# One row preparation at a time, v's sums ahead of q's turning, and PSUM tiles at fixed banks in the second input stage of a transformer block

## The chip, the cores and the metric

The kernel runs on one core of one Trainium2 chip. A core has a matrix engine (TensorE, PE in the profile, with its weight loads shown apart as PEld), a vector engine (VectorE, DVE), a scalar engine (ScalarE, ACT), a general engine (GpSimd, POOL) and a queue that here only issues DMAs (SyncE, SP). Each engine takes its own instructions in their order and waits on semaphores for the others. TensorE writes its results to PSUM, which holds eight banks of 128 x 512 float32 values; all else lies in SBUF or in DRAM.

The metric is the device time of one execution in microseconds (us); lower is better.

## The reference

The reference is one block of a conditioned transformer on x of shape 2 x 2048 x 576 in float32, with 16 heads of 36 values:

```python
mod = jax.nn.silu(c) @ w_ada + b_ada
sh_msa, sc_msa, g_msa, sh_mlp, sc_mlp, g_mlp = jnp.split(mod, 6, axis=1)
xn = _ln(x, 1e-06) * (1 + sc_msa[:, None, :]) + sh_msa[:, None, :]
qkv = (xn @ w_qkv + b_qkv).reshape(B, N, 3, H, hd)
q, k, v = (qkv[:, :, 0], qkv[:, :, 1], qkv[:, :, 2])
q = _ln(q, 1e-05, qn_g, qn_b)
k = _ln(k, 1e-05, kn_g, kn_b)
attn = jax.nn.softmax(jnp.einsum('bqhd,bkhd->bhqk', q, k) * scale, axis=-1)
o = jnp.einsum('bhqk,bkhd->bqhd', attn, v).reshape(B, N, C)
x = x + g_msa[:, None, :] * (o @ w_proj + b_proj)
xn2 = _ln(x, 1e-06) * (1 + sc_mlp[:, None, :]) + sh_mlp[:, None, :]
h = jax.nn.gelu(xn2 @ w1 + b1, approximate=False)
x = x + g_mlp[:, None, :] * (h @ w2 + b2)
```

## The kernel before

The two batch elements go one after the other through three stages: the inputs (normed x times w_qkv, then the norm of each head of q and k), the attention, and the output projection. The MLP follows for both at once. The change touches the input stage of the second element, its border to the attention, and the PSUM pool that this stage shares with the first element's output projection.

**The second input stage** is `in_pairs` (L1327). Tokens come in tiles of 128, sixteen of them. Tiles 0 and 1 are done singly; then seven pairs follow, t0 = 2, 4, ... 14, called pair 2 to pair 14 below. A pair makes three products in the order k, q, v, each of two token tiles by 576 columns. `seven_products` (L1195) computes each from seven smaller matrix products by a Strassen scheme, in four groups: (1,), (2, 6), (5, 7), (4, 3). The figures name the small products. Each group takes one PSUM tile from `s_tile()`, of two banks, so that the four groups of one product fill all eight banks, and group n of a product needs the tile that group n of the product before has left.

**What empties the tiles** is `combined` (L1233): an ACT copy of product 1, and five DVE sums `do[0]` to `do[4]` (L1248 to L1252). `do[0]` reads the group (2, 6). `do[1]` reads both banks of the group (5, 7). `do[2]` reads product 4, `do[3]` product 5 and `do[4]` product 3. So the tile of (5, 7) is free once `do[3]` is done, and that of (4, 3) after `do[4]`.

**What follows for k and q** is `finishing` (L1279): square (ACT, L1287), sum per head (DVE, L1291), root (ACT, L1294), reciprocal (DVE) and scaling (POOL, L1300), and `turned_out` (L1302). The last transposes in blocks of 32 on DVE (L1304) and writes the result to DRAM by eight DMAs (L1307): seven on SP and one on POOL. Then it reads rows back for the attention. For k that is `take_k_block` (L875), called with four tiles in pairs 2, 6 and 10 and with two tiles in pairs 12 and 14; it issues four DMAs on SP (L812 for `km`, L814 for `ke`). For q it is `take_q(0, 0)` in pair 2 alone, eight DMAs on SP. All of these wait until the writes have landed. The names `kt` and `qt` in the code stand for this last step of k and of q.

**A row preparation** is what is left to be done on DVE once the rows are back. For a block of k it is one function: `scaled` of `km` and `parted` of `ke`, four instructions (L847, L847, L856, L857). For q it is two functions: `scaled` of `qm` (one instruction), and `parted` of `qe` (three). The functions wait in the list `taken`.

**The order of the work** is written out by hand in this stage: DVE, SP, POOL and ACT, like PE, take their instructions in the order of the code. In a pair the order on DVE, seen from the lines in `in_pairs`, is this. First come what the pair before left (`rest`: v's `do[2]` to `do[4]` and q's `qt`), then k's five sums, and after q's products k's sum per head, q's `do[0]`, and `kd`. There q's `do[1]` and the call `rows_made()` (L1389) stand, which runs all that `taken` holds; then `kt`, q's `do[2]` to `do[4]`, and after v's products q's sum per head, v's `do[0]`, `qd` and v's `do[1]`. In the last pair `qt` stands ahead of v's `do[2]` to `do[4]` (L1404).

**The border.** The attention's PSUM pool has eight single banks in the place of the four tiles; its first four score matmuls (L1519) take banks 0 to 3. A bank can be written once the last reader of what lay there is done.

Of the kernel before, what the change touches and what calls it, by code (L numbers as in the profile page):

```python
# [8 lines left out]
F32 = mybir.dt.float32  # L9
# [7 lines left out]
P = 128  # L17
# [14 lines left out]
def dit_block(  # L32
# [26 lines left out]
    B, N, C = x.shape  # L59
# [16 lines left out]
    psum = {}  # L76

    @contextmanager
    def psum_pools():
        with (  # L80
# [2 lines left out]
        ):  # L83
            yield

    def s_tile():
        return psum["s"].tile([P, 2, 512], F32, tag="s", name="s")

    def bank():
# [6 lines left out]
    def opened(name, bufs=1, side="left"):  # L96

        stack = ExitStack()
        pool = stack.enter_context(tc.tile_pool(name=name, bufs=bufs, side=side, reuse_waits="tile"))
        return pool, stack.close  # L100

    def opened_psum(**bufs):

        stack = ExitStack()
        for n, count in bufs.items():
            psum[n] = stack.enter_context(
                tc.tile_pool(name=f"ps_{n}", bufs=count, space=PSUM, reuse_waits="tile")
            )

        def close():  # L110
            stack.close()
            for n in bufs:
                del psum[n]

        return close
# [636 lines left out]
    def block_of_small():  # L752
# [13 lines left out]
        def outs_opened():  # L766
            outs, close = opened("outs", side="right")
            held["qo"] = outs.tile([P, NKC, N], F32, name="qo")
            held["spare"] = outs.tile([P, 11, C], F32, name="spare")
            spare[:] = [held["spare"][:, i, :] for i in range(11)]  # L770
            nc.gpsimd.memset(held["spare"][0:1, :, 0:1], 0.0)
            return close
# [294 lines left out]
        def input_modulated(b, xnt):  # L1067
            turned_modulated(xnt, slice(0, P), 0, b)
            return xnt
# [12 lines left out]
        def inputs(b, weights, making, work, xnts, turned, loaded):  # L1082

            wq, wq4, bq = weights
            both, squares, taken = {}, {}, []
# [44 lines left out]
            def product(w, t, ps=None, steps=(0, 1)):  # L1130

                ps = ps or s_tile()
                full, parts, _ = xnts[t]
                for a in range(2):
                    f = slice(w * C + a * HALF, w * C + (a + 1) * HALF)
                    out_a = ps[:, a, :HALF]
                    for k in range(FULL) if 0 in steps else ():
                        nc.tensor.matmul(out_a, full[:, k, :], wq[:, k, f], start=k == 0, stop=False)  # L1138
                    for i in range(2) if 1 in steps else ():
                        nc.tensor.matmul(out_a, parts[:, i, :], wq4[:, f], start=False, stop=i == 1)  # L1140
                return ps
# [35 lines left out]
            def bias_rows():  # L1177

                spread = work.tile([P, 3, 2, HALF], F32R, name="bias_rows")
                ones = work.tile([P, P], F32R, name="ones")  # L1180
                nc.gpsimd.memset(spread.bitcast(F32), 0.0)
                nc.gpsimd.memset(ones.bitcast(F32), 0.0)
                nc.gpsimd.memset(ones[0:2, :].bitcast(F32), 1.0)
                value, up = ended[0:2, :HALF], high[0:2, :HALF]
                for w in range(3):
                    first, second = (bq[0:2, w * C + a * HALF : w * C + (a + 1) * HALF] for a in range(2))
                    nc.vector.tensor_tensor(value, second, first, ALU.subtract)
                    for a, part in enumerate((first, value)):
                        nc.vector.tensor_scalar(up, part, sign_q[0:2, :], None, ALU.mult)
                        nc.vector.scalar_tensor_tensor(  # L1190
                            spread[0:2, w, a, :], part, low_q[0:2, :], up.bitcast(F32), ALU.mult, ALU.add
                        )
                return spread, ones
# [74 lines left out]
            def features_begun(t):  # L1268
                if t < NT and t not in xnts:
                    xnts[t] = input_loaded(turned.pop(t), nc.gpsimd, work if t % 4 == 3 else None)  # L1270

            def pair_opened(w, t0):
                pairs[w] = work.tile([P, 2, C], F32, name="pair", bufs=4)
                both.update({(w, t0 + t): pairs[w][:, t, :] for t in range(2)})
# [46 lines left out]
                return squares_made, summed_up, rooted, divided, turned_out  # L1321

            def rows_made():
                while taken:
                    taken.pop(0)()

            def in_pairs():  # L1327

                sums = work.tile([P, 4, 2, 3, HALF], F32, name="weight_sums")
                less = work.tile([P, 3, HALF], F32R, name="wq4_less")  # L1330
                nc.sync.dma_start(out=less.bitcast(F32), in_=saved["less"])
                for w in (1, 0, 2):
                    nc.sync.dma_start(out=sums[:, :, :, w, :], in_=saved["sums"][:, :, :, w, :])
                spread, ones = bias_rows()

                for w in (1, 0):
                    pair_opened(w, 0)
                features_begun(3)
                k = product(1, 0)
                biased(1, k, 0)  # L1340
                q = product(0, 0)
                biased(0, q, 0)
                v = product(2, 0)
                biased(2, v, 0)
                k = product(1, 1)
                biased(1, k, 1)
                input_modulated(b, xnts[3])
                more = token_sums(2)
                ks, kr, kq, kd, kt = finishing(1, 0)
                ks(), kr(), kq(), kd()  # L1350
                q = product(0, 1)
                biased(0, q, 1)
                qs, qr, qq, qd, qt = finishing(0, 0)
                qs(), qr(), qq()
                kt()
                qd()
                v = product(2, 1)
                biased(2, v, 1)
                rest = [qt]

                for t0 in range(2, NT, 2):
                    last = t0 == NT - 2
                    operands = sums, less, spread, ones, more
                    for t in range(2):
                        features_begun(t0 + 2 + t)

                    pair_opened(1, t0)
                    do, copied = combined(1, t0, seven_products(1, t0, operands))
                    copied()
                    for step in rest:  # L1370
                        step()
                    do[0]()
                    do[1]()
                    do[2](), do[3](), do[4]()
                    ks, kr, kq, kd, kt = finishing(1, t0)
                    ks()

                    pair_opened(0, t0)
                    do, copied = combined(0, t0, seven_products(0, t0, operands))
                    copied()  # L1380
                    kr(), kq()
                    do[0]()
                    kd()
                    if not last:
                        for t in range(2):
                            input_modulated(b, xnts[t0 + 2 + t])
                        more = token_sums(t0 + 2)
                    do[1]()
                    rows_made()  # L1389
                    kt()  # L1390
                    do[2](), do[3](), do[4]()
                    qs, qr, qq, qd, qt = finishing(0, t0)
                    qs()

                    do, copied = combined(2, t0, seven_products(2, t0, operands))
                    copied()
                    qr(), qq()
                    do[0]()
                    qd()
                    do[1]()  # L1400
                    if not last:
                        rest = [*do[2:], qt]
                        continue
                    qt()  # L1404
                    do[2](), do[3](), do[4]()
                    return taken

            modulated = {0}
# [28 lines left out]
            if b > 0:  # L1437
                return in_pairs()
# [57 lines left out]
            taken = key_rows[-2:]  # L1496
# [220 lines left out]
        close_psum = opened_psum(s=4)  # L1717
# [7 lines left out]
        for b in range(B):  # L1725
# [5 lines left out]
                left = inputs(b, weights, making, work, xnts, turned, loaded)  # L1731
            close_weights()
            close_work()
            close_outs = outs_opened()
            att, close_att = opened("att")
            close_psum()
            close_psum = opened_psum(b=8)
# [63 lines left out]
                attend(b, att, hooks, left)  # L1801
            close_att()
            close_psum()
            close_psum = opened_psum(s=4)
            wp, close_wp = opening["wp"]
            if b + 1 < B:
                weights, close_weights, making = kept_weights()
# [85 lines left out]
        for j in range(TPB + 1):  # L1893
            n, i = divmod(j, TPB)
# [172 lines left out]
        close_psum = opened_psum(s=4)  # L2067
# [98 lines left out]
    with tc.If(is_small > 0) as branch:  # L2166
        with tc.manual_schedule(engines={mybir.EngineType.PE}):
            block_of_small()
# [34 lines left out]
```

## Time and profile before

| | us |
|---|---|
| median of three runs | 3138.34 (3137.75 to 3140.68) |
| the profiled execution's own time | 3137.95 |
| its span in the trace | 3136.0 |
| TensorE busy in it | 3103.5 |
| DVE busy | 1569.0 |
| first matmul of the second input stage | at 1085.4 |
| first score matmul of the second attention | at 1291.8 |

Times "at" are us from the start of the span. A row of the timeline gives the start, the duration, the engine, the line, the operation, the tile written and those read, and in brackets how long the engine sat idle before and who ended it; rows of one kind that follow each other are merged with a count (x4), and a matmul of float32 stands there twice. SPq is the queue that issues DMAs: its rows show the issue, not the transfer. A window's row gives the busy time and instructions of each engine, and the clock that TensorE was granted (1.00 is full speed).

### The profile page before, as it was taken

How to read it: one execution, taken by the hardware profiler on the slowest of the kernel's cores; microseconds unless marked ns; L12 is line 12 of the kernel's file. 1: busy time of each engine (PE TensorE's matmuls, PEld its weight loads, DVE VectorE, ACT ScalarE, POOL GpSimd, SP SyncE). 2: the span in 40 equal slices, each digit the busy share in tenths (PEclk: the TensorE clock that was granted, in tenths of full speed). 3: DMA queues.
4: the chain of work that ended last, by engine and by line, in shares of the span. 5: the costliest groups of instructions: out<-in, count | busy, mean ns of one | idle time of the engine just before them, and what ended most of it. 6: DMA issues, size and time to landing. Idle time of an engine off the chain costs nothing. (4 is left out here: it accounts for less than half of the span.)

```text
span 3136.0 us, 47001 instructions
## 1 busy us (share of the span) xinstructions
PE 3103.5 (99%) x17511; PEld 1853.4 (59%) x17511; DVE 1569.0 (50%) x2287; ACT 1477.0 (47%) x2853; POOL 718.7 (23%) x1005
## 2 busy tenths in 40 slices
PE   8999999999999999999999999999999999999999
PEld 6883333333333778533333333368888888777777
DVE  6773444444443556444434444355565553545454
ACT  2336666766667023466666666633565541000000
POOL 4650100132321355200011110013333320212111
PEclk9999999999999999999999999999999999999999
DMA  5773332233342644311122321146554434333331
GB/s 146 188 144 85 104 89 57 70 97 96 91 112 56 223 96 77 84 46 34 46 57 74 85 68 57 56 168 188 159 145 130 128 110 167 106 121 122 113 106 39
DMA packets 294838, 324.65 MB, mean 104 GB/s; under 512 B 168904, under 2 KB 225160, under 8 KB 292488
## 3 DMA queue, kind: packets, MB, share of 16 engines
q1 hardware_dynamic: 246464, 198.32, 22.0%
q0 software_dynamic: 46960, 117.92, 14.4%
q10 hardware_dynamic: 1176, 5.31, 0.5%
q8 instruction: 141, 2.31, 0.3%
q14 instruction: 97, 0.79, 0.1%
HBM read 200.50 MB, written 110.43 MB: 99 GB/s over the span
## 5 line engine op out<-in xcount | busy, mean ns | idle before, releaser
L1523 ACT ACTIVATE pt<-b 128x512 f32<-128x512 f32 x2048 | 1057.3, 610 | 483.8 <-PE b L1532 267.6
L1532 PE MATMUL b<-pt,vt 128*64 128x512 f32 x4096 | 935.0, 598 | 1.8 <-ACT pt L1523 1.8
L1532 PEld LDWEIGHTS b<-pt,vt 128*64 128x64 f32 x4096 | 271.8, 136 | 583.9 <-issue 437.7
L1519 PE MATMUL b<-qm,km 32*128 32x512 f32 x4096 | 564.0, 615 | 3.0 <-issue 3.0
L1584 DVE TENSOR_TENSOR ot<-b,ot 128x512 f32<-128x512 f32 x192 | 132.8, 692 | 587.8 <-PE b L1532 587.8
L1519 PE MATMUL b<-qe,ke 16*128 16x512 f32 x2048 | 421.7, 793 | 0.0
L1519 PEld LDWEIGHTS b<-qm,km 32*128 32x128 f32 x4096 | 192.4, 185 | 272.5 <-ACT pt L1523 210.1
L2115 PE MATMUL s<-ws,as 128*128 128x288 f32 x1440 | 351.8, 406 | 0.0
L2115 PEld LDWEIGHTS s<-ws,as 128*128 128x128 f32 x1440 | 273.6, 190 | 75.6
L1138 PE MATMUL s<-wq,xnt 128*128 128x288 f32 x864 | 228.3, 409 | 2.1 <-ACT xnt L395 2.1
L1551 DVE RECIPROCAL den<-den 128x512 f32<-128x512 f32 x64 | 213.5, 3337 | 11.9 <-DMA den<-den_dram 11.9
L1955 PE MATMUL m<-xnt,wb 128*128 128x256 f32 x864 | 210.6, 379 | 1.9 <-issue 0.9
L1955 PE MATMUL m<-s,wb 128*128 128x256 f32 x864 | 210.0, 379 | 0.0
L1582 DVE COPY ot<-b 128x512 f32<-128x512 f32 x64 | 44.3, 692 | 276.9 <-PE b L1532 276.9
L1138 PEld LDWEIGHTS s<-wq,xnt 128*128 128x128 f32 x864 | 159.1, 191 | 38.1 <-ACT xnt L395 1.6
L1955 PEld LDWEIGHTS m<-s,wb 128*128 128x128 f32 x864 | 164.2, 190 | 22.3
L1519 PEld LDWEIGHTS b<-qe,ke 16*128 16x128 f32 x2048 | 108.1, 184 | 113.5 <-issue 112.7
L1955 PEld LDWEIGHTS m<-xnt,wb 128*128 128x128 f32 x864 | 158.8, 190 | 22.0 <-DVE cs L1989 1.8
L1042 POOL DMA_DIRECT2D turned<-squares x160 | 107.5, 679 | 195.9 <-DVE squares L1037 188.2
L1993 ACT ACTIVATE cs<-cs,b_sb 128x512 f32<-128x512 f32 x144 | 98.9, 719 | 113.1 <-DVE cs L1988 89.4
L1059 ACT ACTIVATE xnt<-xnt,mod 128x128 f32<-128x128 f32 x244 | 100.4, 482 | 101.0 <-DMA weight_sums<-sums_kept 51.4
L2115 PE MATMUL s<-ws,hidden 128*128 128x288 f32 x576 | 142.3, 406 | 0.0
(257 smaller groups left out, 3282.3 us busy)
## 6 DMA issues: line engine op xcount, KB each, us to landing
gelu<-cs SPq DMA_DIRECT2D x144, 256.0 KB
hidden<-gelu SPq DMA_DIRECT2D x16, 2304.0 KB
spare<-in_x_dram POOLq DMA_DIRECT2D x64, 288.0 KB, 3.1
x_dram<-spare POOLq DMA_DIRECT2D x64, 288.0 KB, 2.5
qm<-qk SPq DMA_DIRECT2D x256, 64.0 KB
den<-den_dram SPq DMA_DIRECT2D x128, 128.0 KB
xnt<-turned POOLq DMA_DIRECT2D x56, 256.0 KB, 4.0
turned<-squares POOLq DMA_DIRECT2D x160, 72.0 KB, 2.6
```

The costliest lines, as they stand in the source:

```text
L1042: queue.dma_start(out=by_square[g], in_=squares[g * SQ : (g + 1) * SQ, :].rearrange("p (k j) -> p k j", j=SQ))
L1059: nc.scalar.activation(part, part, AF.Identity, **affine(which, k, b))
L1138: nc.tensor.matmul(out_a, full[:, k, :], wq[:, k, f], start=k == 0, stop=False)
L1519: nc.tensor.matmul(ps, k[r, keys], q[r, :], start=first, stop=not first)
L1523: nc.scalar.activation(pt[:, h, :], banks[2 * c + h], AF.Exp, scale=SCALE)
L1532: nc.tensor.matmul(acc[64 * h : 64 * h + 64, :], vt[:, v0 : v0 + 64], pt[:, h, :], start=pt is pts[0][0], stop=pt is pts[-1][0],)
L1551: nc.vector.reciprocal(den, den)
L1582: nc.vector.tensor_copy(ot, acc)
L1584: nc.vector.tensor_tensor(ot, acc, ot, ALU.add)
L1955: nc.tensor.matmul(out_m[m], wb[:, slot[m], k, f * P : (f + 1) * P], moving[m](k), start=k == 0 and m in (1, 2, 5, 6), stop=k == 1 and m == 1,
L1993: nc.scalar.activation(part, part, AF.Gelu, bias=b1_sb[:, g : g + 1])
L2115: nc.tensor.matmul(ms[m], stationary[m][:, f, :], ws[m][:, f, :], start=(f == 0), stop=(f == HF - 1))
```

## The change

Four edits, all for the second input stage (and, for the pool, the first element's output projection).

- `rows_made` runs one preparation, where it ran all that waited.
- It is called at three places of a pair: between k's `do[0]` and `do[1]`, at the old place after q's `do[1]`, and, but for the last pair, between v's `do[0]` (with `qd`) and `do[1]`. They are called the first, the second and the third place below.
- In the last pair v's `do[2]` to `do[4]` stand ahead of `qt`.
- The pool's four tiles rotated as they came free; now each of four names has its own place, and `s_tile` takes them in turn, downwards: 2, 1, 0, 3, 2 and so on. After the stage (`turns.clear()`) the rotation is as it was.

```diff
+    turns = {}
+
     def s_tile():
+        if "next" in turns:
+            turns["next"] = (turns["next"] - 1) % 4
+            return psum["s"].tile([P, 2, 512], F32, tag=f"s{turns['next']}", name="s")
         return psum["s"].tile([P, 2, 512], F32, tag="s", name="s")
...
             def rows_made():
-                while taken:
+                if taken:
                     taken.pop(0)()
...
                     do[0]()
+                    rows_made()
                     do[1]()
                     do[2](), do[3](), do[4]()
                     ks, kr, kq, kd, kt = finishing(1, t0)
...
                     do[0]()
                     qd()
+                    if not last:
+                        rows_made()
                     do[1]()
                     if not last:
                         rest = [*do[2:], qt]
                         continue
+                    do[2](), do[3](), do[4]()
                     qt()
-                    do[2](), do[3](), do[4]()
                     return taken
...
+            turns.clear()
...
-            close_psum = opened_psum(s=4)
+            close_psum = opened_psum(s=1 if b + 1 < B else 4)
+            if b + 1 < B:
+                for i in range(4):
+                    psum["s"].tile([P, 2, 512], F32, tag=f"s{i}", name="s")
+                turns["next"] = 3
```

The changed kernel's line numbers are 5 higher in this stage (3 more from there on to the attention). How the order moves shows at three places.

Engine DVE, pair 2, from v's first sum on (`vt<-s,one` is v's `do[0]`, `turned_qk` the transposition of `qt`). Before:

```order
L1248 TENSOR_TENSOR vt<-s,one 128x2x8x36
L1298 RECIPROCAL inv<-var 128x32
L1249 TENSOR_TENSOR vt<-s,vt 128x2x8x36
L1250 TENSOR_TENSOR vt<-vt,s 128x8x36
L1251 TENSOR_TENSOR vt<-vt,s 128x8x36
L1252 TENSOR_TENSOR vt<-vt,s 128x8x36
L1304 STREAM_TRANSPOSE turned_qk<-pair 128x1152
L1248 TENSOR_TENSOR pair<-s,one 128x2x288
L1249 TENSOR_TENSOR pair<-s,pair 128x2x288
```

The same stretch with the change, into pair 4:

```order
L1253 TENSOR_TENSOR vt<-s,one 128x2x8x36
L1303 RECIPROCAL inv<-var 128x32
L852 TENSOR_SCALAR km_217<-km_217,gb_at 64x512
L852 TENSOR_SCALAR ended<-ke_219,gb_at 64x512
L861 TENSOR_SCALAR high<-ended,part_232 64x512
L862 SCALAR_TENSOR_TENSOR ke_219<-ended,part_230,high 64x512
L1254 TENSOR_TENSOR vt<-s,vt 128x2x8x36
L1255 TENSOR_TENSOR vt<-vt,s 128x8x36
L1256 TENSOR_TENSOR vt<-vt,s 128x8x36
L1257 TENSOR_TENSOR vt<-vt,s 128x8x36
L1309 STREAM_TRANSPOSE turned_qk<-pair 128x1152
L1253 TENSOR_TENSOR pair<-s,one 128x2x288
```

The four instructions of the k block that was turned earlier in the same pair now stand ahead of v's `do[1]`; before, they stood in pair 4, behind q's `do[1]`. The same holds in pairs 6, 10 and 12 (in pair 12 with 64x256). Right behind the last row shown, the first of q's two preparations now stands, ahead of k's `do[1]`:

```order
L1309 STREAM_TRANSPOSE turned_qk<-pair 128x1152
L1253 TENSOR_TENSOR pair<-s,one 128x2x288
L852 TENSOR_SCALAR qm_218<-qm_218,gb_at 128x512
L1254 TENSOR_TENSOR pair<-s,pair 128x2x288
L1255 TENSOR_TENSOR pair<-pair,s 128x288
```

It uses the rows that this same `qt` sends for. The other half of q's preparation stays at the second place of pair 4.

Engine PE, the border: the first four score matmuls with the semaphores that each waits for (DVE_49, PE_49 and Activation_49 are counters of the engines, the DMAHW ones count transfers). Before:

```order
L1519 MATMUL b<-qm_218,km_217 128x512 [waits DMAHW0_49,DMAHW5_49,DVE_49,PE_49]
L1519 MATMUL b<-qm_218,km_217 128x512 [waits DMAHW2_49,DMAHW7_49,DVE_49,PE_49]
L1519 MATMUL b<-qm_218,km_217 128x512 [waits DMAHW4_49,DMAHW0_49]
L1519 MATMUL b<-qm_218,km_217 128x512 [waits DMAHW6_49,DMAHW2_49,Activation_49]
L1519 MATMUL b<-qe_221,ke_219 128x512 [waits DMAHW1_49]
```

With the change:

```order
L1527 MATMUL b<-qm_218,km_217 128x512 [waits DMAHW5_49,DMAHW0_49,Activation_49]
L1527 MATMUL b<-qm_218,km_217 128x512 [waits DMAHW7_49,DMAHW2_49,DVE_49]
L1527 MATMUL b<-qm_218,km_217 128x512 [waits DMAHW4_49,DMAHW0_49]
L1527 MATMUL b<-qm_218,km_217 128x512 [waits DMAHW2_49,DMAHW6_49,DVE_49,PE_49]
L1527 MATMUL b<-qe_221,ke_219 128x512 [waits DMAHW1_49]
```

The first bank used to hang on v's `do[3]` and the second on `do[4]`. Now the first hangs on the ACT copy of v's product 1, the second on `do[0]`, and the fourth on `do[3]`.

## The prediction

> **What bounds the kernel now.** I read the page first, then the windows, then TensorE's timeline in the second input stage beside those of DVE and SP.
>
> ```profile
> span 3136.0 us, 47001 instructions
> PE 3103.5 (99%) x17511; PEld 1853.4 (59%) x17511; DVE 1569.0 (50%) x2287; ACT 1477.0 (47%) x2853; POOL 718.7 (23%) x1005
> ...
> 1085.40:1288.78 203.38, 199.39 (x919) 161.57 (x917) 125.75 (x191) 61.87 (x132) 97.10 (x116) 0.99 0.46 94
> 1159.47:1163.56 4.09, 4.09 (x11) 3.08 (x12) 2.49 (x4) 1.77 (x3) 0.25 (x2) 0.58 0.80 124
> 1291.78:1296.20 4.42, 4.42 (x29) 4.33 (x32) 1.89 (x5) 2.06 (x4) 2.66 (x5) 0.62 0.96 209
> ```
>
> TensorE sets the time: busy 3103.5 of 3136.0 us. In the whole second input stage (third row) it idles 4.0 us; at the border behind it, 3.0 more. So what the change can win here is small, and every microsecond by which TensorE is newly held up is paid in full. The last two rows are the stretches after its two idle times of over 3 us: the granted clock is 0.58 and 0.62 for some 4 us, which costs 4.09 x 0.42 = 1.7 and 4.42 x 0.38 = 1.7 us each.
>
> ```profile
> 1136.17 1.13 PE L1224 MATMUL s<-wq,xnt 128*128 128x288 f32 x4
> 1138.52 2.10 PE L1224 MATMUL s<-weight_sums,more 128*128 128x288 f32 x8
> 1140.24 0.51 PE L1226 MATMUL s<-bias_rows,ones 128*128 128x288 f32 x1
> ...
> 1141.82 1.13 PE L1224 MATMUL s<-weight_sums,xnt 128*128 128x288 f32 x4
> ...
> 1144.29 1.13 PE L1224 MATMUL s<-wq,xnt 128*128 128x288 f32 x4
> 1152.40 1.13 PE L1224 MATMUL s<-wq,xnt 128*128 128x288 f32 x4
> 1159.47 2.02 PE L1224 MATMUL s<-weight_sums,more 128*128 128x288 f32 x4 [3.59 <-DVE pair L1251]
> ```
>
> Pair 4's k starts at 1136.17, q at 1144.29, v at 1152.40: 8.1 us a product. The group (5, 7) begins with the fifth of the eight matmuls at 1138.52; half of 1140.24 - 1138.52 on, that is 1139.38, 3.2 us after its product's start; it lasts until 1141.82. By then the `do[3]` (L1251) of the product before must be done, or TensorE stands. Pair 4's v should get there at 1155.6 and gets there at 1159.47, as the last row says. With the slow clock, v loses 3.87 + 1.7 = 5.5 us.
>
> **What the change removes.** The reason is in DVE's rows:
>
> ```profile
> 1150.14 0.76 DVE L1249 TENSOR_TENSOR pair<-s,pair 128x576 f32<-128x576 f32 x1 [0.77 <-PE s L1230]
> 1150.81 1.04 DVE L847 TENSOR_SCALAR km<-km,gb_at 64x512 f32<-64x512 f32 x1
> ...
> 1153.66 0.67 DVE L847 TENSOR_SCALAR qm<-qm,gb_at 128x512 f32<-128x512 f32 x1
> 1154.26 0.95 DVE L847 TENSOR_SCALAR ended<-qe,gb_at 128x512 f32<-128x512 f32 x1
> ...
> 1157.13 1.36 DVE L1304 STREAM_TRANSPOSE turned_qk<-pair 128x1152 f32<-128x1152 f32 x1
> 1158.42 0.41 DVE L1250 TENSOR_TENSOR pair<-pair,s 128x288 f32<-128x288 f32 x1
> 1158.87 0.46 DVE L1251 TENSOR_TENSOR pair<-pair,s 128x288 f32<-128x288 f32 x1
> ...
> 1259.39 1.21 PE L1224 MATMUL s<-weight_sums,more 128*128 128x288 f32 x4 [0.27 <-DVE pair L1251]
> ```
>
> A k block costs 1153.66 - 1150.81 = 2.85 us, q's first half 0.60, its second 1157.13 - 1154.26 = 2.87. All three stand ahead of q's `do[3]` in pair 4. In the change only the 2.87 stay there: as in pair 12, where a k block alone leaves a wait of 0.27 (last row). I keep 0.5 for pair 4, which removes 5.0 of its 5.5, and give 0.9 for the small losses of pairs 8 and 12, whose blocks leave that place. So far **-5.9 us**.
>
> **What the moved blocks wait for.** This is the larger part. Each block is now made in the pair that turns it, and its rows must first go to DRAM and come back.
>
> ```profile
> 1127.27 1.38 DVE L1304 STREAM_TRANSPOSE turned_qk<-pair 128x1152 f32<-128x1152 f32 x1 [0.72 <-POOL pair L1300]
> 1133.06 0.34 DVE L1298 RECIPROCAL inv<-var 128x32 f32<-128x32 f32 x1
> 1136.38 0.46 DVE L1250 TENSOR_TENSOR vt<-vt,s 128x288 f32<-128x288 f32 x1 [1.72 <-PE s L1230]
> 1136.87 0.46 DVE L1251 TENSOR_TENSOR vt<-vt,s 128x288 f32<-128x288 f32 x1
> 1137.60 1.37 DVE L1304 STREAM_TRANSPOSE turned_qk<-pair 128x1152 f32<-128x1152 f32 x1
> ...
> 1135.85 0.32 SPq L812 DMA_DIRECT2D km<-qk  x1
> 1136.98 0.43 SPq L812 DMA_DIRECT2D km<-qk  x1
> 1148.62 0.44 SPq L812 DMA_DIRECT2D qm<-qk  x1
> ...
> 1291.03 0.43 SPq L812 DMA_DIRECT2D km<-qk  x1
> ...
> 1294.47 0.42 DVE L847 TENSOR_SCALAR km<-km,gb_at 64x256 f32<-64x256 f32 x1 [2.43 <-DMA km<-qk]
> ```
>
> In pair 2, `kt` ends at 1128.65 and its first read of `km` goes out at 1135.85, 7.2 us on, because the eight writes come first. The second read goes out at 1136.98. The last two rows give what it takes to land: 1294.47 - 1291.03 = 3.44 us, with DVE waiting. So the rows of pair 2 are there at 1140.42. DVE comes to the third place at 1133.40, when the reciprocal is done, and would wait **7.0 us**. Before, it came at 1150.81, and nothing waited.
>
> Behind the wait stand v's `do[1]` to `do[3]`, and for them TensorE. After the rows: 2.85 for the block, 0.67 for `do[1]` (1150.81 - 1150.14), 0.95 for `do[2]` and `do[3]` (1136.38 to 1137.33) and 0.14 to TensorE (1159.47 - 1159.33): 4.6 us, so 1145.0. TensorE wants the tile at 1139.38. A stall of 5.6 us.
>
> Then `qt` follows at 1145.4 and ends at 1146.8. Its rows take longer: before, `qt` ended at 1138.97 and the last read of `qm` went out at 1148.62, landing at 1152.06 by the same 3.44, so 13.1 us after `qt`. (It landed before 1153.66, when DVE used it, which bounds the 13.1 by 14.7.) Now q's first half stands right behind `qt` and k's `do[0]`, and waits until 1159.9. Behind it k's sums: 0.60 + 0.67 + 0.95 + 0.14 later, at 1162.3, q's group (5, 7) may start. Before, it started at 1144.29 + 3.2 = 1147.5. Pairs 2 and 4 together lose **14.8 us**, whatever the clock does between, and **1.7** for the slow clock behind.
>
> Pairs 6, 10 and 12 repeat pair 2 without q's part:
>
> ```profile
> 1190.37 1.13 PE L1224 MATMUL s<-wq,xnt 128*128 128x288 f32 x4
> 1191.14 0.44 SPq L812 DMA_DIRECT2D km<-qk  x1
> 1239.42 1.13 PE L1224 MATMUL s<-wq,xnt 128*128 128x288 f32 x4
> 1239.89 0.44 SPq L812 DMA_DIRECT2D km<-qk  x1
> ...
> 1279.02 0.80 DVE L847 TENSOR_SCALAR km<-km,gb_at 64x256 f32<-64x256 f32 x1
> 1281.09 1.38 DVE L1304 STREAM_TRANSPOSE turned_qk<-pair 128x1152 f32<-128x1152 f32 x1
> ```
>
> Pair 6: rows at 1194.58, the tile free at 1199.2, wanted at 1193.6: 5.6. Pair 10: 1243.33, 1247.9, 1242.6: 5.3. Pair 12 has the short block, 2.07 in place of 2.85 (last two rows), so 4.7 by pair 2's distances. With three times 1.7 for the clock: 15.6 + 5.1 = **20.7 us**.
>
> The prices that are least sure are the landing and the clock.
>
> ```profile
> DMA to landing us min/median/max: 2.6/3.3/3.9
> ```
>
> That is the answer for the reads of `km` that POOL issues near the border: 2.6 to 3.9 us after issue, which with 0.43 of issue time is from 0.4 less to 0.9 more than 3.44; it enters five times. A stall may cost no clock (the 0.27 us wait did not) or twice 1.7. I take the 3.44 and the 1.7, since both were measured behind waits of this kind.
>
> The Trainium skill, "DMA: Bandwidth & Descriptors", section "Anatomy of one DMA", fits a DMA by 2.0 us plus its bytes over 436 GB/s, an estimate of 2.15 us for these 64 KB. By that the sum would be some 6 us lower, 3161; the row of this trace has 3.44 and decides.
>
> **The border and the banks.** The first score matmul starts at 1291.78 although the last product ends at 1288.78:
>
> ```profile
> 1288.14 0.64 PE L1230 MATMUL s<-wq,xnt 128*128 128x288 f32 x2
> ...
> 1289.47 1.38 DVE L1304 STREAM_TRANSPOSE turned_qk<-pair 128x1152 f32<-128x1152 f32 x1 [1.63 <-POOL pair L1300]
> ...
> 1291.59 0.45 DVE L1252 TENSOR_TENSOR vt<-vt,s 128x288 f32<-128x288 f32 x1
> ```
>
> With the sums ahead of `qt`, `do[2]` starts 0.21 after the product (as at 1136.38 after 1136.17), at 1288.99; `do[3]` ends at 1289.94 and is what the fourth bank waits for. The first three banks are free earlier. That is worth 1.7 to 3.0 us; I take **-2.0**, nearer the lower end, as the four score matmuls of a step run beside each other and the last decides. Inside the stage the fixed banks cost nothing: four tiles for four groups, so group n still follows group n, and only their order is turned round. `qt` is later by 1.9 at the border; its rows are of q's tiles 14 and 15, used much later.
>
> **The sum**, from the profiled execution's own 3137.95: -5.9 + 14.8 + 1.7 + 20.7 - 2.0 = +29.3, so 3167.2. The median shown is 0.4 above that execution: **3167 us**, or 0.9% slower. About 0.2% (6.3 us) can be told from no change.
>
> **The rivals.**
>
> *DVE waits, but only for q.* If k's reads came back within the slack, the four third places would cost nothing, and q's wait alone remained. `qt` then ends at 1141.8 (2.85 later than before, behind the block), the rows are there at 1154.9 and q's group starts at 1157.3 in place of 1147.5: +9.8 + 1.7 - 5.9 - 2.0 = +3.6, 3142 us. For it the rows must be there by 1139.38 - 4.6 = 1134.8. Against it: the read is not even issued before 1135.85. 5%.
>
> *Faster.* The spread preparations fill DVE's idle time (busy 125.75 of 203.38 us) and nothing is waited for: -5.9 - 2.0, 3130 us. The point of decision is the landing: by 1133.4 for k, and before `do[1]` of pair 4 for q. It speaks for it that DVE is idle at all three places; against it, the same rows as above. 3%.
>
> *Slower still.* After each wait DVE is late for the next product as well, so that a second stall follows, as the 0.27 after one block alone, and the clock stays low for twice as long: five times 1.7 plus some 2 us, 3178. For it: in pair 4 two stalls already follow each other. Against: after a stall DVE has about 2.4 us of work (`do[4]`, `qt`, `do[0]`) while TensorE needs 2.4 for the group (5, 7) at full clock and 4.1 at the slow one. 9%. The Trainium skill, "TensorE: Matmul & The Clock Gate", Part 1, has the clock halved after an idle window of about 3.4 us and restored after a busy one of that length, windows running freely; an estimate by it is 1.7 to 3.4 us a stall, which would point to this side.
>
> *The fixed banks do not follow the groups*, so that a product's first group waits for the last sum of the one before, `do[4]`. That ends behind `do[3]`'s 1137.33, so at least 1.2 us into the next product: up to 21 times 1.2 more, 3192 us. Against: the order of the first score matmuls shows that each bank still waits for its own reader. 3%.
>
> **How the numbers follow.** The forecast has 80%. Its own range: the landing -0.4 to +0.9 five times, the clock 0 to 3.4 four times in place of 1.7, the border 1 us: 3157 to 3179. Widened for the rival on the slow side and for smaller faults in the waits, 3154 to 3182. Slower by over 0.2% takes the forecast and the last two rivals: 0.92; the first rival gives 0.05 within 0.2%, the second 0.03 faster.
>
> **What would show it.** In the profile after: DVE idle of about 7 us before `km`, ended by the DMA, in pairs 2, 6, 10 and 12, and one before `qm` in pair 4; TensorE idle before the group (5, 7) of the product after each, ended by DVE, some 4.7 to 7.5 us; the granted clock dipping behind each; the stage 31 us longer; no wait of 3.6 in pair 4's v. I am wrong if DVE is not seen waiting for `km` (the rows came sooner than the issue rows say), or if it waits and TensorE does not.

## The result, and the profile after

The changed kernel takes 3164.5 us (median of four runs, 3162.3 to 3168.0) where the kernel before takes 3138.7. The ratio is 1.0082, 95% interval 1.0065 to 1.0100: slower by 0.8%. The forecast was 3167 us, within 3154 to 3182.

The first rows of the page of the changed kernel, and the windows of its second input stage: the whole stage up to the first score matmul, and the 7 us behind each stall of TensorE (busy PE, PEld, DVE, ACT and POOL, then the granted clock).

```profile
span 3164.7 us, 46996 instructions
PE 3112.9 (98%) x17511; PEld 1856.2 (59%) x17511; DVE 1566.2 (49%) x2287; ACT 1477.3 (47%) x2853; POOL 713.5 (23%) x1005
...
1085.40:1318.82 233.42, 209.19 (x919) 167.93 (x917) 122.77 (x191) 61.88 (x132) 96.09 (x116) 0.93 0.40 82
1145.64:1152.64 7.00, 7.00 (x25) 5.51 (x26) 2.15 (x3) 0.00 (x0) 0.71 (x1) 0.74 0.55 86
1160.85:1167.85 7.00, 7.00 (x20) 5.43 (x21) 4.49 (x8) 5.56 (x14) 2.71 (x2) 0.61 0.00 0
1209.38:1216.38 7.00, 7.00 (x22) 5.43 (x23) 2.91 (x4) 0.00 (x0) 0.71 (x1) 0.66 0.56 84
1266.71:1273.71 7.00, 7.00 (x20) 5.41 (x21) 2.90 (x4) 0.00 (x0) 0.71 (x1) 0.61 0.60 87
1295.95:1302.95 7.00, 7.00 (x25) 5.55 (x26) 3.15 (x5) 0.00 (x0) 0.70 (x1) 0.76 0.61 87
```

Both kernels begin the stage at 1085.40. The first score matmul starts at 1318.82 in place of 1291.78, 27.0 us later, and what follows has its old length to within 2 us. So the loss lies in this stage. The five windows give what the slow clock costs behind each stall, (1 - granted) x 7: 1.8, 2.7, 2.4, 2.7 and 1.7 us. With the 24.2 us of stalls that makes 35.5 us; less the 8.6 us that the same stretch lost before (3.59 + 0.27 + 3.00 of waits, 1.7 of slow clock) it is 26.9.

TensorE's timeline, the five rows with a wait and the border:

```profile
1145.64 1.78 PE L1229 MATMUL s<-weight_sums,more 128*128 128x288 f32 x3 [5.97 <-DVE vt L1256]
1160.85 2.26 PE L1229 MATMUL s<-weight_sums,more 128*128 128x288 f32 x4 [5.09 <-DVE pair L1256]
1209.38 2.26 PE L1229 MATMUL s<-weight_sums,more 128*128 128x288 f32 x4 [5.05 <-DVE vt L1256]
1266.71 2.26 PE L1229 MATMUL s<-weight_sums,more 128*128 128x288 f32 x4 [6.10 <-DVE vt L1256]
1295.95 2.20 PE L1229 MATMUL s<-weight_sums,more 128*128 128x288 f32 x4 [2.02 <-DVE vt L1256]
...
1318.25 0.64 PE L1235 MATMUL s<-wq,xnt 128*128 128x288 f32 x2
1318.82 1.81 PE L1527 MATMUL b<-qm,km 32*128 32x512 f32 x7
```

Each stall stands before the group (5, 7) and ends with the `do[3]` (L1256 now) of the product before: four times v's, once k's. The stalls of 3.59 and 0.27 us of before are gone, and so is the border's 3.00.

What DVE waited for in the same stretch, from its timeline, and the two rows of SP's queue that belong to pair 2 and to q:

```profile
1127.28 1.38 DVE L1309 STREAM_TRANSPOSE turned_qk<-pair 128x1152 f32<-128x1152 f32 x1 [0.71 <-POOL pair L1305]
1133.08 0.34 DVE L1303 RECIPROCAL inv<-var 128x32 f32<-128x32 f32 x1
1141.03 0.54 DVE L852 TENSOR_SCALAR km<-km,gb_at 64x512 f32<-64x512 f32 x1 [7.61 <-DMA km<-qk]
...
1145.78 1.37 DVE L1309 STREAM_TRANSPOSE turned_qk<-pair 128x1152 f32<-128x1152 f32 x1
1158.44 0.55 DVE L852 TENSOR_SCALAR qm<-qm,gb_at 128x512 f32<-128x512 f32 x1 [10.65 <-DMA qm<-qk]
...
1204.68 0.54 DVE L852 TENSOR_SCALAR km<-km,gb_at 64x512 f32<-64x512 f32 x1 [6.60 <-DMA km<-qk]
...
1261.71 0.55 DVE L852 TENSOR_SCALAR km<-km,gb_at 64x512 f32<-64x512 f32 x1 [7.35 <-DMA km<-qk]
...
1292.03 0.42 DVE L852 TENSOR_SCALAR km<-km,gb_at 64x256 f32<-64x256 f32 x1 [4.35 <-DMA km<-qk]
```

```profile
1137.10 0.43 SPq L817 DMA_DIRECT2D km<-qk  x1
...
1156.18 0.44 SPq L817 DMA_DIRECT2D qm<-qk  x1
```

Five waits for DMAs, at the five places that the prediction named, and behind each a stall of TensorE.

### The profile page after: what moved, and what is told of

Same layout as the page of the kernel before. It is cut to its first block, busy times and chain, and to the rows that moved or that the text cites. A ratio compares the mean times of both kernels' runs of the same rounds, so it can differ in the third digit from the quotient of the medians.

```text
span 3164.7 us, 46996 instructions
## 1 busy us (share of the span) xinstructions
PE 3112.9 (98%) x17511; PEld 1856.2 (59%) x17511; DVE 1566.2 (49%) x2287; ACT 1477.3 (47%) x2853; POOL 713.5 (23%) x1005
## 3 DMA queue, kind: packets, MB, share of 16 engines
q1 hardware_dynamic: 246464, 198.32, 21.8%
```

## The experiments

All kernels differ from one of the two in a few lines; their times stand beside the kernel before, which was run with each group again (3138.2 to 3138.5 us).

**The spread alone, and the other two edits alone.** The first kernel has `if taken` and the three places, but the old last pair and the old pool. The second has only the new last pair and the fixed tiles.

> The kernel before with only the first two edits: one preparation at a time, at three places; the last pair and the PSUM tiles as before. Theory of late rows (DVE waits for rows that were sent for in the same pair): the five stalls of the changed kernel, 24.2 us and some 10 us of slow clock, stay, and the border's 3.0 us comes back: 3164.5 + 3.0 = 3167 us. Theory of banks (the fixed tiles, taken downwards, share in the stalls): without them most of the loss is gone, below 3150 us.

> The kernel before with only the last two edits: v's sums ahead of q's turning in the last pair, and the fixed PSUM tiles. Theory of late rows: these edits cost nothing in the stage and win the border's idle time, which was 3.0 us before and is not there in the changed kernel: 3138.7 - 3.0 = 3135.7 us, the stage's stalls as before (3.6 and 0.3 us). Theory of banks: slower than before, up to 25 us.

Measured: 3154.5 us for the spread (ratio 1.0050, 1.0036 to 1.0064), and 3135.1 for the other two edits (0.9990, 0.9981 to 0.9999). So the other two edits win 3.3 us when they are alone, as I expected, and the spread alone costs 16.0, not 29. That fits neither of my two theories: it is 12.5 us under the first and above the second's 3150. The stalls are there, but smaller than in the change. If the two halves simply added up, they would make 3151, and the change makes 3164.5. They hurt each other.

**The tiles.** The changed kernel without its fourth edit looks for these 13 us:

```diff
-            close_psum = opened_psum(s=1 if b + 1 < B else 4)
-            if b + 1 < B:
-                for i in range(4):
-                    psum["s"].tile([P, 2, 512], F32, tag=f"s{i}", name="s")
-                turns["next"] = 3
+            close_psum = opened_psum(s=4)
```

> The changed kernel without its fourth edit, the PSUM tiles rotating as before; the other three stay. The spread alone took 3154.5 us, 10 us less than the whole change. Theory of tiles that adapt (in rotation k's group (5, 7) takes, after a late v, the tile that k's own product 1 has just left, so that TensorE goes on for one group before it stands): 3154.5 less some 1.5 us of the border, 3153 us, with stalls of v's tiles shorter by 2 us or more each than the 5.97, 5.05, 6.10 and 2.02 of the changed kernel. Theory that the third edit and the fixed tiles do nothing inside the stage and the spread alone was quick for another reason: 3162 to 3165 us.

Measured: 3154.3 us (1.0049, 1.0035 to 1.0063), 10.2 less than the whole change, as the theory of tiles that adapt had it. TensorE's waits in the stage, and three of the rows behind them:

```profile
PE s L1229 <- DVE vt L1256: 9.0, 3, 3.6
PE s L1229 <- DVE pair L1256: 7.8, 2, 7.6
...
1145.11 1.27 PE L1229 MATMUL s<-weight_sums,xnt 128*128 128x288 f32 x4 [2.73 <-DVE vt L1256]
1160.37 2.26 PE L1229 MATMUL s<-weight_sums,more 128*128 128x288 f32 x4 [7.60 <-DVE pair L1256]
...
1308.35 1.09 PE L1527 MATMUL b<-qm,km 32*128 32x512 f32 x5 [1.44 <-issue]
```

Behind v the stall stands before another matmul: `weight_sums,xnt` is the first of product 4, that is of the group (4, 3), and not product 5 (`weight_sums,more`). The program says why: which tile a group gets is chosen when the program is built and stands in it. These are the first matmuls of products 5 and 4 in pair 4's k, with what each waits for; first with rotating tiles, then with fixed ones:

```
L1229 MATMUL s<-weight_sums,more 128x288 [waits Activation_49]
L1229 MATMUL s<-weight_sums,xnt 128x288 [waits DVE_49,PE_49]

L1229 MATMUL s<-weight_sums,more 128x288 [waits DVE_49,PE_49]
L1229 MATMUL s<-weight_sums,xnt 128x288 [waits DVE_49,PE_49]
```

In rotation this group waits for ACT: only a tile of group (1,) is released by ACT, and v's has already gone to k's own group (1,), so it is the tile that k's product 1 has just left. TensorE gets a whole group further before it needs v's `do[3]`. This holds in four products (the k of pairs 4, 8, 12 and 14), all of them behind a v with a preparation at the third place. In before no group (5, 7) does so, and in the kernel below that has rotating tiles but no third place, none does either. So "four tiles for four groups, group n follows group n" is no property of the pool. It is how the rotation falls out where no preparation stands ahead of v's sums, and fixing the tiles takes away its other way out. The stalls behind v are 2.73, 2.65, 3.59 and none, for 5.97, 5.05, 6.10 and 2.02 with fixed tiles; q's is 7.60 for 5.09, as nothing lies before it to shorten it. That is 16.8 us of stalls in the stage (9.0 + 7.8) for 24.2, and 6.3 us of slow clock for 11.3: 12.4 us less in the stage, from which the border's 1.4 us of idle time goes off again: 11.0, where the two profiled executions are 11.4 us apart and the medians 10.2.

**Late rows or work in the wrong place?** The block also is 2.85 us of DVE work ahead of `do[1]`. The next kernel keeps the work where it is and takes the wait away: in pairs 6, 10 and 12 `kt` first sends for rows of tiles 0 to 3 (0 and 1 in pair 12), which were written long before, then turns and writes. The block is then made from rows of other tokens.

```diff
+                    early = w == 1 and t0 in (6, 10, 12)
+                    if early:
+                        taken.append(take_k_block(t0 - 2 if t0 < 12 else t0, t0 + 2, 0))
                     turned_qk = work.tile([P, 2 * C], F32, name="turned_qk", bufs=2)
                     nc.vector.transpose(turned_qk, pair)
```

> The changed kernel, but in pairs 6, 10 and 12 the block's rows are read from token tiles 0 to 3 (0 and 1 in pair 12), written long before, and sent for ahead of this pair's turning; so the block is computed from rows of other tokens. DVE's work, its places and the number of DMAs stay. Theory of late rows: the rows land some 4 us after kt begins and DVE, 6 us behind kt, does not wait; the stalls of 5.05, 6.10 and 2.02 us go with their slow clock, 13.2 + 5.7 us: 3164.5 - 18.9 = 3145.6 us; the two of pair 4 (5.97 and 5.09) stay. Theory of work in the wrong place: the stalls stay, 3164.5 us.

Measured: 3142.7 us (1.0015, 1.0006 to 1.0024), 21.8 less than the change, where 18.9 was expected for late rows and nothing for work in the wrong place. DVE's rows at the third places of pairs 6, 10 and 12, and TensorE's waits:

```profile
1199.59 0.44 DVE L852 TENSOR_SCALAR km<-km,gb_at 64x512 f32<-64x512 f32 x1
1199.95 2.34 DVE L852 TENSOR_SCALAR ended<-ke,gb_at 64x512 f32<-64x512 f32 x1
...
1248.40 2.72 DVE L852 TENSOR_SCALAR km<-km,gb_at 64x512 f32<-64x512 f32 x1
...
1273.50 2.32 DVE L852 TENSOR_SCALAR km<-km,gb_at 64x256 f32<-64x256 f32 x1
```

```profile
PE s L1230 <- DVE vt L1257: 5.8, 2, 5.2
PE s L1230 <- DVE pair L1257: 4.6, 1, 4.6
```

No wait for a DMA is left there, and of the three stalls (13.2 us) 0.5 us. The 5.2 and the 4.6 are those of pair 4, which were left as they were. So the rows were late, and the place by itself costs next to nothing, even with an instruction that takes 2.7 us in place of 0.55.

**q alone.** The changed kernel without the first place:

```diff
                     do[0]()
-                    rows_made()
                     do[1]()
```

> The changed kernel without the first place: q's two parts are made at the second and the third place of pair 4, the blocks of k at the third places as in the changed kernel. Theory of late rows: the wait of 10.65 us for qm at the first place of pair 4 goes or shrinks to under 2 us, and with it the stall of 5.09 us and its slow clock of 2.1: 3164.5 - 7.2 = 3157.3 us; the other four stalls stay. Theory that the stalls come from one another (the first one makes DVE late for the rest): the stall of pair 4's q stays in part, 3161 us or more.

Measured: 3154.5 us (1.0051, 1.0037 to 1.0065): 10.0 less, where 7.2 was expected. The row of `qm` and the waits:

```profile
1158.24 1.04 DVE L852 TENSOR_SCALAR qm<-qm,gb_at 128x512 f32<-128x512 f32 x1
...
PE s L1229 <- DVE vt L1256: 15.7, 4, 5.9
```

No wait for `qm`, no stall ended by a sum of k. The 5.09 and its 2.7 of slow clock make 7.8. The two profiled executions are further apart than the medians, 13.3 us, since the four stalls that stay were smaller as well: 15.7 us for 19.1, and 5.2 of slow clock for 8.6. Of the 3.4 us of stalls 2.6 are in pair 4's k, 3.37 for 5.97. That stall comes before the place that was taken out, so it is no effect of the edit; it varies with how fast the rows come back (below).

**Without the third place.** Blocks of k are then made at the first place of the next pair:

```diff
                     qd()
-                    if not last:
-                        rows_made()
                     do[1]()
```

> The changed kernel without the third place: a block of k is then made at the first place of the next pair, some 10 us later, behind k's do[0]; q's two parts at the second place of pair 4 and the first of pair 6. As many instructions on DVE as in the changed kernel. Theory of late rows: all five stalls go, since the rows have been there for 5 us or more at each place: 3138.7 - 5.9 - 3.0 = 3130 us, faster than both; DVE has no wait for km or qm of over 0.5 us. Theory of work in the wrong place (2.85 us of DVE work ahead of a product's do[1] is by itself what TensorE waits for): four stalls of some 5 us move from the product after v to the product after k, 3155 to 3165 us.

Measured: 3128.8 us (0.9969, 0.9957 to 0.9981): faster than both kernels, by 9.7 and 35.7 us. The stage with the first 3.1 us of the attention, and the place where pair 2's block now stands:

```profile
1085.40:1286.00 200.60, 200.58 (x946) 163.08 (x945) 125.73 (x195) 62.70 (x134) 97.37 (x119) 1.00 0.47 97
```

```profile
1140.28 0.76 DVE L1253 TENSOR_TENSOR pair<-s,one 128x576 f32<-128x576 f32 x1 [0.78 <-PE s L1229]
1140.95 0.53 DVE L852 TENSOR_SCALAR km<-km,gb_at 64x512 f32<-64x512 f32 x1
```

TensorE is busy 200.58 of 200.60 us at full clock. The block is that of the change; only its place is one product later, and the rows are there (but for one wait of DVE of 0.95 us for `ke`, at 1239.96, which TensorE does not feel). q's two parts come later too, at the second place of pair 4 and the first of pair 6, and find their rows as well. Against the kernel with the border's two edits alone (3135.1) the spread wins 6.3 us here; what each of the two shifts gives by itself was not tried.

The same without the fixed tiles:

> The changed kernel without the third place and with rotating PSUM tiles, that is without the fourth edit. Theory that the tiles matter in the stage only where a sum is late: no sum is late here, so the stage is as without the third place, and only the border's 1.4 us come back: 3128.8 + 1.5 = 3130.3 us, no stall inside the stage. Theory that fixed tiles cost by themselves: below 3128.

Measured: 3129.9 us (0.9975, 0.9965 to 0.9984), with no stall in the stage and 1.1 us at the border. Where no sum is late, the tiles change nothing that can be seen but the border.

**Which of the two border edits wins?** Each alone on the kernel before:

> The kernel before with the fourth edit alone, the fixed PSUM tiles. If the order of the banks is what the border hangs on (the first score matmul had to wait for v's do[3], now only the fourth does): the border's 3.0 us go, 3135.5 us. If it hangs on the sums, which still stand behind q's turning: nothing moves, 3138.5 us. In the stage no change by either.

> The kernel before with the third edit alone, v's last three sums ahead of q's turning in the last pair. If the border hangs on the sums: do[2] and do[3] stand 1.9 us earlier, 3138.5 - 1.7 = 3136.8 us, with some 1.3 us of idle time left. If it hangs on the order of the banks: 3138.5 us.

Measured: 3137.9 us for the tiles (0.9999, 0.9990 to 1.0008) and 3136.7 for the last pair (0.9994, 0.9985 to 1.0003); both together were 3135.1. Neither alone can be told from no change, but the rows show what each does. With the tiles alone:

```profile
1290.38 1.13 PE L1524 MATMUL b<-qm,km 32*128 32x512 f32 x6
1293.44 0.66 PE L1524 MATMUL b<-qm,km 32*128 32x512 f32 x1 [1.93 <-issue]
```

The first three banks start at once and the fourth waits 1.93 us for the sums behind `qt`. With the last pair alone:

```profile
1291.42 1.28 PE L1524 MATMUL b<-qm,km 32*128 32x512 f32 x5 [1.08 <-issue]
```

The first bank hangs on `do[3]` and starts 1.08 us late. With both, the sum that is early is also the one that the last bank needs, and nothing waits.

**A short stall and the clock.** DVE is held back by idle copies at the third place, in the kernel that has no preparations there:

```diff
+                    for _ in range({4: 8, 6: 9, 8: 10, 10: 11, 12: 12}.get(t0, 0)):
+                        nc.vector.tensor_scalar(ended, ended, 1.0, 0.0, ALU.mult, ALU.add)
                     do[1]()
```

> The kernel without the third place, with DVE held back by idle copies of 128x512 (0.59 us each) ahead of v's do[1]: 8, 9, 10, 11 and 12 of them in pairs 4, 6, 8, 10 and 12, that is 4.7, 5.3, 5.9, 6.5 and 7.1 us. DVE comes to that place 5.98 us before TensorE wants the tile of (5, 7), and needs 1.76 us behind it (0.67 + 0.95 + 0.14), so 4.2 us are free: stalls of 0.5, 1.1, 1.7, 2.3 and 2.9 us in the next pair's k, 8.5 us in all, ended by v's do[3]. It asks what a short stall costs in clock. If any stall of about 1 us or more brings the slow clock for some 4 us: four times 1.8, so 3128.8 + 8.5 + 7.2 = 3144.5 us. If only a stall near 3 us does: 3128.8 + 8.5 + 1.8 = 3139 us.

Measured: 3147.8 us (three runs, 3145.3 to 3152.6). The stalls and the windows behind them:

```profile
1166.20 1.60 PE L1229 MATMUL s<-weight_sums,more 128*128 128x288 f32 x4 [1.90 <-DVE vt L1256]
1194.43 1.21 PE L1229 MATMUL s<-weight_sums,more 128*128 128x288 f32 x4 [1.98 <-DVE vt L1256]
1221.86 2.26 PE L1229 MATMUL s<-weight_sums,more 128*128 128x288 f32 x4 [2.85 <-DVE vt L1256]
...
1280.49 1.21 PE L1229 MATMUL s<-weight_sums,more 128*128 128x288 f32 x4 [2.75 <-DVE vt L1256]
```

```profile
1166.20:1173.20 7.00, 7.00 (x25) 5.53 (x26) 5.00 (x8) 0.00 (x0) 0.71 (x1) 0.76 0.56 86
1194.43:1201.43 7.00, 7.00 (x33) 5.74 (x34) 6.34 (x11) 0.35 (x1) 0.71 (x1) 1.00 0.56 84
1221.86:1228.86 7.00, 7.00 (x26) 5.58 (x27) 3.33 (x5) 0.00 (x0) 0.71 (x1) 0.78 0.55 84
...
1280.49:1287.49 7.00, 7.00 (x33) 5.73 (x34) 5.76 (x11) 0.53 (x1) 0.70 (x1) 1.00 0.58 86
```

The five sets of copies took 6.2 to 8.0 us, 0.60 to 0.78 a copy and not 0.59, so the stalls add up to 13.0 us and not to 8.5. The mean hides that in each set one copy took 2.2 to 2.7 us and the others 0.36 to 0.74 (the last section comes back to it). Neither theory of the clock holds: 1.90 us cost 1.7 of clock, 1.98 nothing, 2.85 cost 1.5, 2.75 nothing. Three of the five paid (the one of 3.56 us, not shown, too): with 13.0 + 3 x 1.6 on 3128.8 it comes to 3146.6.

## Why the prediction was right, point by point

The terms of its sum against the profiled execution after:

| term | forecast | measured | from |
|---|---|---|---|
| old stalls of pairs 4, 8 and 12 | -5.9 | -5.6 | 3.59 + 0.27 + 1.7 of clock, no rest left |
| pairs 2 and 4 | +14.8 | +13.4 | q's group (5, 7) at 1160.85 for 1147.5 |
| stalls of pairs 6, 10 and 12 | +15.6 | +13.2 | 5.05 + 6.10 + 2.02 |
| slow clock behind four of them | +6.8 | +9.5 | 2.7 + 2.4 + 2.7 + 1.7 |
| border | -2.0 | -3.0 | 3.00 before, none now |
| sum | +29.3 | +27.5 | the first score matmul is 27.0 later |

That the sum is so close is in part luck. The first and the fourth term were 3.0 us too low, the other three together 4.8 too high. And one gain was left out: the slow clock behind the border's wait, 1.7 us by the prediction's own row (0.62 over 4.42 us), goes with the wait; the 7 us from 1318.82 on are granted 1.00. With it the terms make 25.8, which is what the medians are apart. The two profiled executions are 28.1 apart, as the attention and the rest happened to take some 3 us longer than that in the one of the changed kernel.

- **What bounds the kernel**: held. DVE was busy 122.77 of 233.42 us and TensorE lost all the same, through waits.
- **The moved blocks wait for their rows**: held, and shown: without the wait, with the work in place, the stalls were gone. In pair 2 the forecast had rows at 1140.42 and TensorE at 1145.0; they were 1141.03 and 1145.64, the wait 7.61 for 7.0 and the stall 5.97 for 5.6.
- **The landing, 3.44 us each time**: it was one measurement, from a read of 32 KB, and the five spread around it: 3.93 (1141.03 - 1137.10), 3.07, 4.05, 1.99 and for `qm` 2.26 (1158.44 - 1156.18). The 1.99 is the one of 32 KB, but the 2.26 is of 64 KB, so the size alone does not explain it. The Trainium skill, "DMA: Bandwidth & Descriptors", section "Anatomy of one DMA", gives the fit that the prediction used for DMAs that GpSimd issues, and these went out on SP's queue. The estimate by it, 2.15 us, is near two of the five; the other three lie between 3.07 and 4.05.
- **q's rows, 13.1 us after `qt`**: 11.3 (1158.44 - 1147.15). From that come 1.4 us of pairs 2 and 4.
- **Pair 12's stall, 4.7**: the worst term, 2.02 measured. Its rows landed 1.45 us sooner than by 3.44, and `kt` and the issue of its reads lay 8.5 us apart, not the 9.8 of pair 2. I had taken pair 2's distances for it.
- **The clock, 1.7 a stall**: too little. The stalls of 5 to 6 us cost 1.8 to 2.7, the one of 2 us 1.7. What the *slower still* rival said of the clock was in part right; its other half, a second stall behind each, was not seen.
- **The border**: -2.0 was too careful; the whole 3.0 of idle time went, and 1.7 of slow clock with it. It took both edits, as the two runs with one of each show.
- **"Inside the stage the fixed banks cost nothing"**: this step was wrong. It compared the fixed tiles with a rotation that follows the groups, which is the rotation of before. Beside the late sums of the spread, the rotation would have been another one, and the fixed tiles cost 12 us of the stage against it, 10 with what they win at the border. The sum came out right since the stalls were worked out for tiles in fixed order, which the change has: +29.3 as a whole was right, but its split was not. From the kernel with the border's two edits alone to the whole change it is 29.4 us (3164.5 - 3135.1); about 16 of them belong to the spread and 13 to the tiles beside it. My rival on the banks (3192 us) looked for another fault, and the waits speak against that one as expected.
- *Only q waits* (3142) and *faster* (3130): out, by the four waits for `km`. But 3130 is what the same spread gives without the third place: 3128.8.

## What to carry to other kernels

Before a preparation is moved to where an engine has time, count from the instruction that sends for its data to the place: here a round trip through DRAM took 10.5 to 13.8 us, the new place lay 6 us behind, and one product (8 us) further on the same work was free and the kernel faster than both. An engine that takes its work in order passes such a wait on to all that is queued behind it: the waits were what was paid for, not the 2.85 us of work. And when tiles are given fixed places, the program loses the rotation's way round a late reader: try the two edits together and apart, since their times did not add up (-3.3 and +16.0 alone, +25.8 together).

## What the runs showed of the hardware that I had not expected

- **A stall of about 2 us may or may not cost clock.** Over all runs in which windows were read, stalls up to 1.44 us cost none; of the ten between 1.90 and 2.75 five (1.90, 1.93, 2.02, 2.65, 2.73) cost 1.5 to 1.7 us and five (1.98, 2.00, 2.02, 2.44, 2.75) cost nothing; each of 2.85 us and more cost 1.4 to 3.1. The Trainium skill, "TensorE: Matmul & The Clock Gate", Part 1, has windows of some 3.4 us that run freely, and a drop after one idle window. That two stalls of 2.02 us differ agrees with windows that run freely; that 1.90 us are enough does not agree with a whole idle window. What decides in this range stays open.
- **The round trip through DRAM varies by several us for the same DMAs.** From the start of `kt` in pair 2 to the first use of its rows it took 13.8 us in the changed kernel (1127.28 to 1141.03), 12.8 with rotating tiles and 10.8 without the first place. In the last the seven writes of SP were issued in 3.64 us, in the changed kernel in 4.86.
- **One DVE instruction took 2.2 to 2.7 us in place of some 0.5 while POOL worked.** In the run with older rows the `km` instruction at 1248.40 ended at 1251.12, and POOL's scaling of the pair ran from 1248.68 to 1250.82; the one at 1199.95 (2.34) ran beside POOL's from 1199.75 to 1202.01. In the changed kernel DVE comes to the same instructions after POOL is done, and they take 0.54. In the run with idle copies the same shows five times over: in each set the second copy, beside which POOL's scaling of the pair ran (2.14 to 2.18 us), took 2.2 to 2.7 us, the first 0.36 and the later ones 0.43 to 0.74. Not every instruction is held: without the third place v's `do[1]`, a sum, took 0.76 us at 1134.42, with POOL's scaling running from 1134.00 to 1136.13. That it is the other engine was not tested by a run in which POOL's work is moved away. The Trainium skill, "GPSIMD Engine Reference", section 1, "Specifications", says that GpSimd shares its SBUF interfaces with VectorE, with contention for some of VectorE's instructions; these rows agree.
